# Attention slots of a decoder layer: projections and out-projections issued ahead of the weighted values, and the general arm's transfers on ScalarE's queue

## The chip, the core and the metric

The kernel runs on one core of one Trainium2 chip. A core has TensorE (PE; its weight loads are listed apart as PEld), VectorE (DVE), ScalarE (ACT), GpSimd (POOL) and SyncE (SP), which run side by side and wait for one another through semaphores. Each engine takes its instructions in the order in which the program lists them. The metric is the time of one execution on the device in microseconds (us), lower being better.

## The reference, cut to what matters

One pre-norm decoder layer on `x` of 4 batches, 1024 tokens and 256 features, all fp32: windowed self-attention, cross-attention to 77 context tokens, and a feed-forward block whose activations and weights are rounded to int8 steps. Both attentions have 16 heads of 16 features.

```python
x = x + attn(layernorm(x))                        # self, windows of 128 tokens
x = x + xattn(layernorm(x), ctx_1024, mask)       # cross, 77 keys
x = x + ffn(layernorm(x))

def attn(x):                                      # per batch and head
    q, k, v = split(x @ w_qkv)
    # a chunk of 128 queries sees its own chunk and the one before, causally
    scores = q_chunk @ concat(k_prev_chunk, k_chunk).T / 4
    return merge(softmax(where(causal, scores, -inf)) @ concat(v_prev, v)) @ w_out

def xattn(x, ctx):
    q, k, v = x @ Wq.T + bq, ctx @ Wk.T + bk, ctx @ Wv.T + bv
    return merge(softmax(where(mask == 0, -inf, q @ k.T / 4)) @ v) @ Wo.T + bo

def ffn(x):
    h = fake_quant(silu(fake_quant(x) @ Wg.T) * (fake_quant(x) @ Wu.T))
    return h @ Wd.T          # one quantisation scale over all of x, one over all of h
```

The mask that is drawn here has the same row for every query.

## The kernel before, in words

The attention part treats eight jobs in turn: self-attention ("S") of batches 0, 1 and 2, cross-attention ("X") of batch 0, S of batch 3, X of batches 1, 2 and 3. A job is cut into units `(job, g, o, u)`: `g` and `o` pick four heads, whose score products run in four row groups of TensorE at once, and `u` picks two tiles of 128 tokens (S, four values) or half of the tokens (X, two values). That makes 96 units.

The work is written out as a loop over **slots**, one for each unit. `tc.manual_schedule(engines=None)` keeps every engine's instructions in the order in which this loop emits them. A slot of the steady state emits, in this order:

1. for the units that `values_of` lists, **the weighted values**: `weighted_values` (32 or 40 products into the bank `ps_av`, L854, for S; 4 long ones, L864, for X; then a VectorE transpose from the bank, L878), `normalise` (reciprocal L886 and product L888 on VectorE) and, for `o == 1`, `by_features` (a second VectorE transpose, L900). An S job has these in every second slot, an X job in every slot;
2. **the tasks** that are due: `project` (q and k, `ps_p`, L304, taken out of the bank by two ScalarE instructions, L363, L367 or L369), `values` (`ps_v`, one ScalarE copy, L696), `out_project` (`ps_op`, added to `x` by VectorE, L918), `normed_T` (the transposes `ps_t`), and the weights' preparation. `next_in` picks them by due slot and by a cost limit for each slot;
3. **pieces set beside** (`beside`): VectorE work on statistics (L192, L194), on the quantisation of the feed-forward weights (L598 to L608) and on the third norm's maxima (L949);
4. `put_maxima`, where a group of heads is complete: its negated maxima go through TensorE, a ScalarE copy and four transfers on SyncE's queue into the spare rows of `q`;
5. `maxima` for the unit five slots ahead (`LEAD = 5`): scores into the four banks `sc_n` (L725, L740), reduced by VectorE to maxima (L755: eight pairs of instructions for S; L766: four for X);
6. `weights` of the slot's own unit: scores into the four banks `sc_t` (L810, L839), exponentials by ScalarE (L820, L842), a causal selection by GpSimd (L824).

All PSUM banks come from one pool of eight under one tag, `tag="b"`, and are handed out in turn. So the first bank that a slot asks for is the one that held the first `sc_n` of the slot before, the second one that of the second `sc_n`, and so on; the last ones that it asks for (the last `sc_t`) are those that it took first.

The last `LEAD` slots (`tail`) and the slot after the last unit have code of their own.

`values` writes into five tiles `vtiles`, used in turn; `values` for the second pair of token tiles of a job goes into the tile that the job before last read in its weighted values.

Whether all mask rows are alike is found out at the start; `tc.If(rows_alike != 0)` then runs `attention(True)` and `feed_forward()`, or, in the general arm, `attention(False)` and `feed_forward()`. Both arms are in the program, and the first is the one that runs here. Transfers are issued by SyncE but for the last two output blocks, which ScalarE issues (L1522), and for accumulating ones by GpSimd.

Of the kernel before, what the change touches and what calls it, by code (L numbers as in the profile page):

```python
# [25 lines left out]
def decoder_layer(  # L26
# [175 lines left out]
    with ExitStack() as att:  # L202
# [204 lines left out]

        begun = dict(turn)
        begin.close()

        def attention(alike):
            turn.update(begun)
            arm = ExitStack()
            wp = arm.enter_context(tc.tile_pool(name="wa", bufs=1))
            stage = arm.enter_context(tc.tile_pool(name="stage", bufs=2))
# [21 lines left out]
            def prep_cross():  # L437
# [4 lines left out]
                def load_biases():  # L442
                    with nc.allow_non_contiguous_dma(reason="256-element biases"):
                        for name, src in (("q", bq), ("k", bk)):
                            raws[name] = small.tile([P, NP], F32, name="raw_b")
                            nc.sync.dma_start(out=raws[name], in_=src.rearrange("(g p) -> p g", p=P))
                    nc.sync.dma_start(out=bv_b, in_=bv.partition_broadcast(SK))
                    nc.sync.dma_start(out=bo_b, in_=bo.partition_broadcast(P))

                def biases():  # L450
                    for name, dst, by, plus in (("q", bq_p, qrows, nextrow), ("k", bk_p, rows, onerow)):
# [6 lines left out]
                def transposed(w, name, dst=None):  # L458
                    def load():
                        raws[name] = stage.tile([P, NC, D], F32, name="raw_w", tag="stage")  # L460
                        nc.sync.dma_start(out=raws[name], in_=w.rearrange("(c p) i -> p c i", p=P))

                    def turn():
                        wx[name] = dst
                        if dst is None:
                            wx[name] = work.tile([P, NC, D], F32, name=name, tag="wkv", bufs=1)
                        for ic in range(NC):
                            ps = bank("ps_w")
                            for oc in range(NC):
                                nc.tensor.transpose(  # L470
                                    ps[:, oc * P : (oc + 1) * P],
                                    raws[name][:, oc, ic * P : (ic + 1) * P],
                                    ident,
                                )
                            nc.vector.tensor_copy(wx[name][:, ic, :], ps[:, 0:D])

                    return [load, turn]

                def load_context():
                    raws["c"] = stage.tile([SK, B, D], F32, name="craw", tag="stage")  # L480
                    nc.sync.dma_start(out=raws["c"], in_=ctx_in.rearrange("b k d -> k b d"))

                def context():
                    for c in range(NC):
# [51 lines left out]

                def load_row():
                    raws["m"] = stage.tile([P, SK], I32, name="mrow", tag="stage")
                    nc.sync.dma_start(out=raws["m"], in_=mask[0, :].partition_broadcast(P))

                def add_row():

                    row = raws["r"] = stage.tile([P, SK], F32, name="brow", tag="stage")
                    nc.vector.tensor_scalar(row, raws["m"], 0.0, NEG, ALU.is_equal, ALU.mult)
                    least = small.tile([P, 1], F32, name="least")
                    nc.vector.tensor_reduce(least, row, AX.X, ALU.max)
                    nc.vector.tensor_scalar(least, least, -NEG, None, ALU.mult)
                    nc.vector.tensor_tensor(nokey, least, least, ALU.subtract)
                    for o in range(NS):
                        for g in range(NP):  # L550
                            at = (1 - o) * HD + 1
                            nc.sync.dma_start(
                                out=kx[at : P : SL, g, o, :].rearrange("j (b k) -> j b k", b=B),
                                in_=row[0:NJ].unsqueeze(1).to_broadcast([NJ, B, SK]),
                            )

                def load_mask():
                    raws["m"] = stage.tile([P, NT, SK], I32, name="mraw", tag="stage")
                    nc.sync.dma_start(out=raws["m"], in_=mask.rearrange("(t p) k -> p t k", p=P))

                def mask_bias():
                    nc.vector.tensor_scalar(mb_n, raws["m"], 0.0, NEG, ALU.is_equal, ALU.mult)
# [47 lines left out]
            def prep_ffn():  # L610


                def rows_of(w, dst, sc, f):
                    kept = {}

                    def load():
                        kept["raw"] = stage.tile([P, D], F32, name="raw_f", tag="stage")
                        if f < NF - 1:
                            nc.sync.dma_start(out=kept["raw"], in_=w[f * P : (f + 1) * P, :])
                        else:  # L620
                            for r in (0, HR):
                                nc.sync.dma_start(out=kept["raw"][r : r + HR], in_=w[f * P :, :])

                    def scale():
                        kept["i"] = row_scale(kept["raw"], P, sc[:, f : f + 1])

                    def quant():
                        kept["q"] = stage.tile([P, D], BF16, name="q_f", tag="stage_q")
                        quantise_rows(kept["raw"], P, kept["i"], kept["q"])

                    def turn():
                        ps = ps_b.tile([P, NC, P], BF16, name="ps_f", tag="b")
                        for c in range(NC):
                            nc.tensor.transpose(
                                ps[:, c, :], kept["q"][:, c * P : (c + 1) * P], ident_bf
                            )
                        nc.vector.tensor_copy(dst[:, :, f * P : (f + 1) * P], ps)

                    return [load, scale, quant, turn]

                def down(c):
                    kept = {}

                    def load():
                        kept["raw"] = stage.tile([P, FF], F32, name="raw_d", tag="stage")
                        nc.sync.dma_start(out=kept["raw"], in_=w_down[c * P : (c + 1) * P, :])

                    def scale():
                        kept["i"] = row_scale(kept["raw"], P, dsc[:, c : c + 1])
# [124 lines left out]
            def put_maxima(job, g, o):  # L774

                ps = bank("ps_mx")
                nc.tensor.transpose(
                    ps[: NJ * NT, :P], job.mx[g, o].rearrange("p j t -> p (j t)"), ident
                )
                mxT = work.tile([NJ * NT, P], F32, name="mxT", tag="mxT", bufs=2)  # L780
                nc.scalar.copy(mxT, ps[: NJ * NT, :P])
                for j in range(NJ):
                    row = j * SL + (1 - o) * HD
                    nc.sync.dma_start(
                        out=job.q[g, o][row : row + 1, :],
                        in_=mxT[j * NT : (j + 1) * NT, :],
                    )
# [335 lines left out]
            for j, job in enumerate(jobs):  # L1123
# [58 lines left out]
                            values_of.setdefault(at, []).append((job, g, o, hf))  # L1182
                if S_:
                    for t2 in range(NT // 2):
                        a, by = ((-3, -1) if j else (-1, -1), (-1, 1), (3, 3), (4, 4))[t2]
                        task(t0 + a, t0 + by, 1.0, values, job, t2)
                then = jobs[j + 1].kind if j + 1 < len(jobs) else ""
                for hf in range(NH):
# [25 lines left out]
            for slot in range(first, last):  # L1214
# [6 lines left out]
                if slot == N:  # L1221
# [11 lines left out]
                        while after:  # L1233
                            after.pop(0)()
                    last_project(jobs[-1])
                else:
                    for args in values_of.get(slot, ()):
                        weighted_values(*args)
                        normalise(*args, tail)
                        if not tail:  # L1240
                            by_features(*args)
                spent = 0.0
                cap = 1.35 if now and ahead else 2.3
                while t := next_in(tasks, slot, spent, cap):
                    spent += t[3]
                    fn, args = t[4:]
                    fn(*args)
                    if fn is out_project:
                        job, hf, t2 = args
                        if job.kind == "X" and t2 == HT // 2 - 1:  # L1250
                            third_norm(job.b, hf, slot)
                spent = 0.0
                while t := next_in(beside, slot, spent, 1.2):
                    spent += t[3]
# [25 lines left out]
        def feed_forward():  # L1280
# [149 lines left out]
            def rows_out(t0):  # L1430
                b, t = divmod(t0, NT)
                return out[b, t * P : (t + 2) * P, :].rearrange("(t p) d -> p t d", p=P)
# [1 line left out]

            added_there = {t0 for t0 in range(0, B * NT - 4, 2) if t0 % 4 == 0}
            for t0 in sorted(added_there):
                nc.sync.dma_start(out=rows_out(t0), in_=xb[t0 // NT][:, t0 % NT : t0 % NT + 2, :])

            ins = [Input(0), Input(1)]
            ins[0].quantise(2, HT, nc.vector)  # L1440
# [56 lines left out]
            def down(q, t0, nt):  # L1497
                odd = t0 // HT % 2
                for t2 in range(nt // 2):
# [19 lines left out]
                        nc.gpsimd.dma_start(out=rows_out(t0 + 2 * t2), in_=y, accum_op=ALU.add)  # L1519
                    else:  # L1520
                        nc.vector.tensor_tensor(y, y, xb[b][:, t : t + 2, :], ALU.add)
                        (nc.scalar if t0 + 2 * t2 >= B * NT - 4 else nc.sync).dma_start(  # L1522
                            out=rows_out(t0 + 2 * t2), in_=y
                        )


            parts = [(0, 2), (2, 2)] + [(i * HT, HT) for i in range(1, NB - 1)]
# [67 lines left out]
```

## Time and profile before

| | us |
|---|---|
| median of 3 runs | 665.53 (665.24 to 666.23) |
| the profiled execution's own time | 663.93 |
| its span, first to last instruction | 662.1 |
| TensorE / VectorE / ScalarE / GpSimd busy | 613.3 / 542.7 / 367.6 / 268.8 |
| granted TensorE clock, mean | 0.99 |

The profile is of one execution. "Busy" is the union of an engine's instructions; matmuls are pipelined and their ends are modelled. In the views of waits each line names who waited, for whom, the total in us, how often, and the longest. In the timeline each row has the start in us, the length, the engine, the line of the kernel, the operation, its tiles, how many were merged, and the idle time before it with what ended it. The attention slots fill about 31 to 540 us of the span, the feed-forward block the rest.

### The profile page before, as it was taken

To read this page: it belongs to the slowest core of one execution; us is meant where nothing else is said; L and a number is where in the kernel's file an instruction comes from. 1 tells how busy PE (TensorE), PEld (TensorE's weight loads), DVE (VectorE), ACT (ScalarE), POOL (GpSimd) and SP (SyncE) were. 2 spreads that over 40 slices of the span, in tenths; PEclk is the share of its full clock that TensorE was granted. 3 is DMA by queue.
4 is the path that set the end of the run, shared out by engine and by line. 5 is a ranking of instruction groups with operands and counts; after the bars stand their busy time and mean duration, and the time that the engine had idled before them with its cause. 6 is when DMAs were issued, how large, how long until landed. Compare 5 with 4: busy or idle time off the path is not lost.

```text
span 662.1 us, 20220 instructions
## 1 busy us (share of the span) xinstructions
PE 613.3 (93%) x7857; PEld 350.9 (53%) x7862; DVE 542.7 (82%) x1922; ACT 367.6 (56%) x672; POOL 268.8 (41%) x520
## 2 busy tenths in 40 slices
PE   9899999999999999999999999999999997787775
PEld 6456566566555665654446666544443445333564
DVE  6878778868779799678997996897978787889896
ACT  2365564644555634645565366447556475788392
POOL 3164533647234667650044867526611141111032
PEclk9999999999999999999999999999999999989899
DMA  8100100000000000000000000000000020000057
GB/s 291 48 4 15 38 3 2 18 5 5 18 27 10 12 2 19 9 15 14 8 10 11 12 24 26 5 3 4 3 2 4 4 96 17 1 0 1 0 97 165
DMA packets 18080, 17.43 MB, mean 26 GB/s; under 512 B 2998, under 2 KB 17335, under 8 KB 17975
## 3 DMA queue, kind: packets, MB, share of 16 engines
q1 hardware_dynamic: 15239, 13.69, 6.4%
q0 software_dynamic: 1904, 1.84, 2.1%
q8 instruction: 64, 1.05, 0.7%
q10 hardware_dynamic: 832, 0.53, 0.3%
q14 instruction: 41, 0.34, 0.2%
HBM read 9.47 MB, written 6.03 MB: 23 GB/s over the span
## 4 chain that ended last, share of the span: by engine, by line
PE 61%; DVE 25%; ACT 7%; issue 5%; POOL 1%; DVEq 0%; ACTq 0%
PE ps_p L304 13%; PE ps_av L854 8%; PE sc_t L810 7%; PE sc_n L725 7%; PE ps_op L304 6%; PE ps_av L864 4%; PE sc_t L839 3%; DVE junk L755 3%; PE ps_v L304 3%; PE sc_n L740 3%; DVE bnst L192 2%; DVE o_sb L878 2%; ACT shared L369 2%; PE ps_idle L117 2%; DVE aT L900 2%
## 5 line engine op out<-in xcount | busy, mean ns | idle before, releaser
L755 DVE CUSTOM_DVE_ANT_0 junk<-sc_n,cboth 128x256 bf16<-128x256 f32 (+1 forms) x512 | 172.3, 402 | 35.1 <-PE sc_n L725 35.1
L820 ACT ACTIVATE pt<-sc_t 128x512 f32<-128x512 f32 (+1 forms) x256 | 125.4, 577 | 85.3 <-PE sc_t L810 85.3
L824 POOL TENSOR_SCALAR_AFFINE_SELECT pt<-pt 128x256 f32<-128x256 f32 x256 | 102.2, 407 | 116.1 <-ACT pt L820 105.5
L810 PE MATMUL sc_t<-shared 32*128 32x256 f32 (+1 forms) x1024 | 87.9, 377 | 1.4 <-DVE vx L530 0.3
L842 ACT ACTIVATE ptx<-sc_t 77x512 f32<-77x512 f32 x128 | 65.2, 596 | 37.0 <-PE sc_t L839 37.0
L725 PE MATMUL sc_n<-shared 32*128 32x256 f32 (+1 forms) x1024 | 73.6, 387 | 3.0 <-ACT shared L369 1.6
L810 PEld LDWEIGHTS sc_t<-shared 32*128 32x128 f32 x1024 | 65.5, 185 | 13.6 <-ACT shared L367 3.2
L320 POOL TENSOR_SCALAR xn<-x,mv,rs 128x256 f32<-128x256 f32 x56 | 69.6, 1249 | 0.0
L160 POOL TENSOR_SCALAR ve<-mv 128x4 f32<-128x4 f32 x20 | 4.6, 232 | 153.8 <-DVE mv L194 153.7
L878 DVE STREAM_TRANSPOSE o_sb<-ps_av 128x512 f32<-128x512 f32 x63 | 45.0, 714 | 24.4 <-PE ps_av L854 14.3
L304 PE MATMUL ps_p<-shared,w_s 128*32 128x512 f32 x512 | 60.9, 595 | 3.4 <-DVE mx L766 1.6
L725 PEld LDWEIGHTS sc_n<-shared 32*128 32x128 f32 x1024 | 45.7, 184 | 32.3 <-DVE mx L755 10.8
L854 PE MATMUL ps_av<-pt,vt 128*32 128x256 f32 (+1 forms) x1152 | 59.3, 349 | 3.0 <-DVE mx L755 2.6
L766 DVE TENSOR_REDUCE mx<-sc_n 128x4 f32<-128x308 f32 x128 | 51.8, 466 | 8.5 <-PE sc_n L740 8.3
L854 PEld LDWEIGHTS ps_av<-pt,vt 128*32 128x32 f32 x1152 | 34.9, 110 | 31.5 <-DVE mx L755 6.4
L839 PE MATMUL sc_t<-shared,kx 32*77 32x512 f32 x256 | 45.9, 599 | 0.0
L755 DVE DVE_READ_ACCUMULATOR2_ANT mx<- 128x1 f32 x512 | 42.4, 83 | 0.1
L864 PE MATMUL ps_av<-ptx,vx 77*32 77x512 f32 x256 | 35.9, 605 | 3.4 <-DVE mx L766 2.5
L363 ACT ACTIVATE shared<-ps_p,bq_p,qrows 128x512 f32<-128x512 f32 x32 | 23.1, 773 | 26.0 <-PE ps_p L304 26.0
L740 PEld LDWEIGHTS sc_n<-kx,shared 32*128 32x128 f32 x1024 | 31.7, 186 | 10.2 <-DVE rec L886 1.7
L740 PE MATMUL sc_n<-kx,shared 32*128 32x77 f32 x1024 | 36.5, 277 | 0.0
L1406 ACT ACTIVATE act<-pg,gsc 128x512 f32<-128x512 f32 x44 | 29.2, 687 | 11.4 <-PE pg L1391 6.3
(201 smaller groups left out, 984.8 us busy)
## 6 DMA issues: line engine op xcount, KB each, us to landing
x<-in_x_dram SPq DMA_DIRECT2D x8, 512.0 KB
shared<-mxT SPq DMA_DIRECT2D x128, 4.0 KB
out_dram<-x SPq DMA_DIRECT2D x7, 256.0 KB
out_dram<-shared POOLq DMA_DIRECT2D x7, 256.0 KB, 4.6
out_dram<-shared SPq DMA_DIRECT2D x7, 256.0 KB
w_s<-in_L_attn_w_qkv_dram SPq DMA_DIRECT2D x2, 384.0 KB
raw_d<-in_L_ffn_w_down_dram SPq DMA_DIRECT2D x2, 352.0 KB
raw_f<-in_L_ffn_w_gate_dram SPq DMA_DIRECT2D x5, 128.0 KB
```

The costliest lines, as they stand in the source:

```text
L304: nc.tensor.matmul(out[r], lhsT[:, r], rhs, skip_group_check=True, **on)
L320: eng.tensor_scalar(xn, xb[job.b][:, t, :], job.st[hf].mv[:, i, 0:1], job.st[hf].rs[:, i : i + 1], ALU.subtract, ALU.mult,)
L725: nc.tensor.matmul(banks[j][:, (i + 1) * 2 * P - n : (i + 1) * 2 * P], q[r, t * P : (t + 1) * P], k[r, k0 * P : k0 * P + n], start=True, s ...
L740: nc.tensor.matmul(banks[j][:, i * SK : (i + 1) * SK], q[r, t * P : (t + 1) * P], k[r, :], start=alike, stop=alike or i == HT - 1,)
L755: nc.vector.tensor_tensor_reduce(out=junk[:, 2 * P - n :], in0=banks[j][:, (i + 1) * 2 * P - n : (i + 1) * 2 * P], in1=cboth[:, 2 * P - n ...
L810: nc.tensor.matmul(banks[j][:, w : w + n], k[r, t * P : (t + 1) * P], q[r, t * P : t * P + n], start=True, stop=True,)
L820: nc.scalar.activation(pt.rearrange("p i a q -> p (i a q)")[:, :w], banks[j][:, :w], AF.Exp)
L824: nc.gpsimd.affine_select(out=pt[:, :, 0, :], in_=pt[:, :, 0, :], compare_op=ALU.is_ge, fill=0.0, base=0, pattern=[[0, 2], [1, P]], channe ...
L839: nc.tensor.matmul(banks[j][:SK], k[r, :], q[r, s], start=alike, stop=True)
L842: nc.scalar.activation(pt, banks[j][:SK], AF.Exp)
L854: nc.tensor.matmul(ps[j * SL : (j + 1) * SL, (a0 - t0) * P : (a1 - t0) * P], slot_of(job.vs[kb // 2][:, kb % 2], heads[j]), job.pts[g, o, ...
L864: nc.tensor.matmul(ps[j * SL : (j + 1) * SL, :], slot_of(vx[:, job.b], heads[j]), job.pts[g, o, j, hf], start=True, stop=True,)
```

## The change

- In the steady state the weighted values of a slot (`weighted_values`, `normalise`, `by_features`) are emitted after the slot's tasks. They still stand ahead of the pieces set beside, of `put_maxima`, `maxima` and `weights`. The tail is as it was.
- The task `values` for the second pair of token tiles may be done in slot 0 or 1 of its job and no earlier (before: from one slot ahead of it).
- A variable `queue_of` holds the queue for transfers: SyncE's in the arm that runs here, ScalarE's in the general arm. Every `nc.sync.dma_start` of `attention` and `feed_forward` goes through it. With that the last two output blocks of the arm that runs go by SyncE.

```diff
+        queue_of = [nc.sync]
 
         def attention(alike):
             turn.update(begun)
+            queue_of[0] = nc.sync if alike else nc.scalar
...
-                    nc.sync.dma_start(
+                    queue_of[0].dma_start(
                         out=job.q[g, o][row : row + 1, :],
                         in_=mxT[j * NT : (j + 1) * NT, :],
                     )
...
                     for t2 in range(NT // 2):
-                        a, by = ((-3, -1) if j else (-1, -1), (-1, 1), (3, 3), (4, 4))[t2]
+                        a, by = ((-3, -1) if j else (-1, -1), (0, 1), (3, 3), (4, 4))[t2]
                         task(t0 + a, t0 + by, 1.0, values, job, t2)
...
                     last_project(jobs[-1])
-                else:
+                elif tail:
                     for args in values_of.get(slot, ()):
                         weighted_values(*args)
                         normalise(*args, tail)
-                        if not tail:
-                            by_features(*args)
                 spent = 0.0
                 cap = 1.35 if now and ahead else 2.3
                 while t := next_in(tasks, slot, spent, cap):
...
                             third_norm(job.b, hf, slot)
+                if not tail:
+                    for args in values_of.get(slot, ()):
+                        weighted_values(*args)
+                        normalise(*args, tail)
+                        by_features(*args)
                 spent = 0.0
                 while t := next_in(beside, slot, spent, 1.2):
                     spent += t[3]
...
                         nc.vector.tensor_tensor(y, y, xb[b][:, t : t + 2, :], ALU.add)
-                        (nc.scalar if t0 + 2 * t2 >= B * NT - 4 else nc.sync).dma_start(
-                            out=rows_out(t0 + 2 * t2), in_=y
-                        )
+                        queue_of[0].dma_start(out=rows_out(t0 + 2 * t2), in_=y)
```

More of the change, by code (lines that the diff above doesn't have):

```diff
@@ L445, in load_biases @@
                             raws[name] = small.tile([P, NP], F32, name="raw_b")
-                            nc.sync.dma_start(out=raws[name], in_=src.rearrange("(g p) -> p g", p=P))
-                    nc.sync.dma_start(out=bv_b, in_=bv.partition_broadcast(SK))
-                    nc.sync.dma_start(out=bo_b, in_=bo.partition_broadcast(P))
+                            queue_of[0].dma_start(out=raws[name], in_=src.rearrange("(g p) -> p g", p=P))
+                    queue_of[0].dma_start(out=bv_b, in_=bv.partition_broadcast(SK))
+                    queue_of[0].dma_start(out=bo_b, in_=bo.partition_broadcast(P))
                 def biases():
@@ L460, in load @@
                         raws[name] = stage.tile([P, NC, D], F32, name="raw_w", tag="stage")
-                        nc.sync.dma_start(out=raws[name], in_=w.rearrange("(c p) i -> p c i", p=P))
+                        queue_of[0].dma_start(out=raws[name], in_=w.rearrange("(c p) i -> p c i", p=P))
                     def turn():
@@ L480, in load_context @@
                     raws["c"] = stage.tile([SK, B, D], F32, name="craw", tag="stage")
-                    nc.sync.dma_start(out=raws["c"], in_=ctx_in.rearrange("b k d -> k b d"))
+                    queue_of[0].dma_start(out=raws["c"], in_=ctx_in.rearrange("b k d -> k b d"))
                 def context():
@@ L538, in load_row @@
                     raws["m"] = stage.tile([P, SK], I32, name="mrow", tag="stage")
-                    nc.sync.dma_start(out=raws["m"], in_=mask[0, :].partition_broadcast(P))
+                    queue_of[0].dma_start(out=raws["m"], in_=mask[0, :].partition_broadcast(P))
                 def add_row():
@@ L558, in load_mask @@
                     raws["m"] = stage.tile([P, NT, SK], I32, name="mraw", tag="stage")
-                    nc.sync.dma_start(out=raws["m"], in_=mask.rearrange("(t p) k -> p t k", p=P))
+                    queue_of[0].dma_start(out=raws["m"], in_=mask.rearrange("(t p) k -> p t k", p=P))
                 def mask_bias():
@@ L618, in load @@
                         if f < NF - 1:
-                            nc.sync.dma_start(out=kept["raw"], in_=w[f * P : (f + 1) * P, :])
+                            queue_of[0].dma_start(out=kept["raw"], in_=w[f * P : (f + 1) * P, :])
                         else:
                             for r in (0, HR):
-                                nc.sync.dma_start(out=kept["raw"][r : r + HR], in_=w[f * P :, :])
+                                queue_of[0].dma_start(out=kept["raw"][r : r + HR], in_=w[f * P :, :])
                     def scale():
@@ L645, in load @@
                         kept["raw"] = stage.tile([P, FF], F32, name="raw_d", tag="stage")
-                        nc.sync.dma_start(out=kept["raw"], in_=w_down[c * P : (c + 1) * P, :])
+                        queue_of[0].dma_start(out=kept["raw"], in_=w_down[c * P : (c + 1) * P, :])
                     def scale():
@@ L783, in put_maxima @@
                     row = j * SL + (1 - o) * HD
-                    nc.sync.dma_start(
+                    queue_of[0].dma_start(
                         out=job.q[g, o][row : row + 1, :],
@@ L1436, in feed_forward @@
             for t0 in sorted(added_there):
-                nc.sync.dma_start(out=rows_out(t0), in_=xb[t0 // NT][:, t0 % NT : t0 % NT + 2, :])
+                queue_of[0].dma_start(out=rows_out(t0), in_=xb[t0 // NT][:, t0 % NT : t0 % NT + 2, :])
             ins = [Input(0), Input(1)]
```

## The prediction

> **What bounds the kernel now.** I read the page's busy shares first, then the attention stretch of the table by windows, then the timeline slot by slot.
>
> ```profile
> PE 613.3 (93%) x7857; PEld 350.9 (53%) x7862; DVE 542.7 (82%) x1922; ACT 367.6 (56%) x672; POOL 268.8 (41%) x520
> ```
> ```profile
> 32.00:540.00 508.00, 492.50 (x6936) 274.63 (x6933) 416.14 (x1645) 280.61 (x553) 237.08 (x463) 1.00 0.05 14
> ```
>
> In the attention slots TensorE shows 492.5 us busy of 508 and VectorE 416.1. Only 15.5 us look idle, but "busy" also covers matmuls that wait inside a group: the groups of `sc_t` take between 1.0 and 2.0 us for the same work. So I measure a slot from the start of its first product to the start of the next slot's. This is a common slot with weighted values and a projection:
>
> ```profile
> 119.16 1.94 PE L854 MATMUL ps_av<-pt,vt 128*32 128x128 f32 x40
> ...
> 120.92 1.90 PE L304 MATMUL ps_p<-shared,w_s 128*32 128x512 f32 x16
> 121.22 0.72 DVE L878 STREAM_TRANSPOSE o_sb<-ps_av 128x512 f32<-128x512 f32 x1 [0.59 <-PE ps_av L854]
> ...
> 122.72 0.71 DVE L900 STREAM_TRANSPOSE aT<-aN 128x512 f32<-128x512 f32 x1
> ...
> 122.75 1.15 PE L725 MATMUL sc_n<-shared 32*128 32x256 f32 x16
> 122.94 1.45 ACT L369 ACTIVATE shared<-ps_p,onerow,rows 128x512 f32<-128x512 f32 x2 [1.96 <-PE ps_p L304]
> ...
> 123.71 1.85 PE L810 MATMUL sc_t<-shared 32*128 32x256 f32 x16
> 123.91 0.42 DVE L755 CUSTOM_DVE_ANT_0 junk<-sc_n,cboth 128x256 bf16<-128x256 f32 x1 [0.48 <-PE sc_n L725]
> ...
> 125.49 1.92 PE L304 MATMUL ps_p<-shared,w_s 128*32 128x512 f32 x16
> ```
>
> Two things are to be seen. First, VectorE's chain for the weighted values (121.22 to 123.33: transpose, reciprocal, product, second transpose) lies wholly beside the projection and the scores; VectorE even waits 0.48 us for `sc_n`. Secondly, `sc_t` runs late: its last bank is the one that the projection used, and ScalarE empties that only at 124.39. Scores and `sc_t` take 122.75 to 125.49, 2.74 us; in slots where nothing waits they take 0.97 + 1.03 = 2.00 (those that end in `ps_v`, as from 98.52 to 104.11). So 0.74 us are lost here.
>
> The second reading is a slot in which, today, no task stands behind the weighted values:
>
> ```profile
> 282.79 1.72 PE L854 MATMUL ps_av<-pt,vt 128*32 128x256 f32 x32
> ...
> 284.61 0.72 DVE L878 STREAM_TRANSPOSE o_sb<-ps_av 128x512 f32<-128x512 f32 x1 [1.51 <-PE ps_av L854]
> ...
> 284.66 1.13 PE L740 MATMUL sc_n<-kx,shared 32*128 32x77 f32 x32
> ...
> 286.11 0.71 DVE L900 STREAM_TRANSPOSE aT<-aN 128x512 f32<-128x512 f32 x1
> ...
> 287.09 0.57 DVE L608 CAST q_f<-w 128x256 bf16<-128x256 int8 x1
> ...
> 287.58 1.61 DVE L766 TENSOR_REDUCE mx<-sc_n 128x4 f32<-128x308 f32 x4
> ...
> 288.10 1.50 PE L304 MATMUL ps_p<-shared,w_s 128*32 128x512 f32 x12 [1.61 <-DVE mx L766]
> ```
>
> The scores are ready by 285.8, but VectorE must first finish the chain (284.61 to 286.74) and the piece set beside (to 287.58). The next slot's first product needs the first `sc_n` bank, so TensorE stands still for 1.61 us until the first reduction is done. That is the order that the change gives to every such slot.
>
> **The change part by part.**
>
> *The weighted values behind the tasks.* The products are the same, so TensorE's own work costs nothing more. The moved steps issue no transfer, nothing on ScalarE and, outside the tail, nothing on GpSimd, so those queues and SyncE's keep their order. On VectorE the transpose L878 now waits for a product that ends later by the tasks' length; behind it queue the rest of the chain, the pieces beside and the reductions, and for the first reduction waits TensorE's next slot (and later `put_maxima`).
>
> I count the wait of each slot after the change from rows. From the end of the weighted values to the start of VectorE's chain: 0.26 us (S; 121.22 less 119.16 + 1.75, L878 only; 0.13 in X with its short products). The chain: 0.72 + 0.25 + 0.42 and gaps = 1.45 us for `o == 0`, 2.15 with L900. The pieces beside: 0.85 (statistics), 0.7 to 0.8 (row scale), 0.65 (L607 and L608), 1.4 (maxima L949), as the slot has them. From the first reduction's start to the next slot's first product: 0.82 us in S (two pairs of L755, then the hand-over), 0.51 in X (287.58 to 288.10). Against this, TensorE itself needs 2.0 us from the end of the weighted values to the end of the slot, 2.2 in X with `put_maxima`, 1.9 in S with it.
>
> There are 53 slots in the steady state with weighted values and tasks. In four classes, the mean wait after, with the pieces beside summed from VectorE's rows between chain and first reduction:
>
> - S, short chain, 15 slots: 0.26 + 1.45 + 0.44 + 0.82 - 1.94 = 1.03; before 0.23
> - S, long chain, 15: 0.26 + 2.15 + 0.55 + 0.82 - 1.94 = 1.84; before 0.54
> - X, short chain, 13: 0.14 + 1.47 + 0.95 + 0.51 - 2.07 = 1.00; before 0.46
> - X, long chain, 10: 0.14 + 2.16 + 1.11 + 0.51 - 2.07 = 1.85; before 0.67
>
> The sum is 15.5 + 27.6 + 13.0 + 18.5 = 74.6 us of waits after. Those of before in the same slots, slot length less unhindered length, are 3.5 + 8.1 + 6.0 + 6.7 = 24.3. The difference is **+50.3 us**. What the change takes away is in it: 12.4 us of the 24.3 are the 19 slots that end in a projection, whose bank ScalarE will now empty under the weighted values. The 0.74 at 119.16 goes, and 0.26 + 2.15 + 0.82 - 2.00 = 1.23 comes: what is late next is VectorE.
>
> The sum's bounds: if half of the 38 us of pieces beside found cover, 19 less, +31; a slot in which a projection already waits 1.7 us inside (476.61 to 485.58) may give that back. Upwards stands the clock:
>
> ```profile
> 64.90:71.00 6.10, 6.02 (x83) 3.90 (x79) 5.28 (x29) 2.32 (x5) 4.09 (x9) 0.72 0.02 4
> ```
>
> Here the granted clock was 0.72 over 6.1 us, which is half speed for 3.4 us, right after the slot from 62.38 to 67.36 that lost 2.98 us; slots that lost 1.3 to 1.5 show no such drop. Thirteen of the slots above come to 2.0 to 2.55 us, in between. If each brought such a stretch, 13 x 1.7 = 22 us more at most. I take zero, since most are nearer to 1.45 and 2.0 than to 2.98, and keep half of it for the range. [...]
>
> *`values` no earlier than slot 0.* Four products of 1.85 us with a ScalarE copy of 0.59 move by a slot or two, for instance from 109.26 to 119.16. The work is the same, and TensorE and ScalarE do it under the same scores: nothing, within 0.5 us each way. Both slots keep their chain, so a wait in the one is as long as I counted.
>
> *The queue variable.* In the arm that runs it changes the last two output blocks alone. ScalarE issues these now in 0.40 us each, SyncE takes 0.37. SyncE leaves the arm at 655.3 and its next instruction stands at 659.7, 4.3 us for a taken jump, hidden while the last blocks land. After the change it leaves about 658.0. With the same 4.3 us it would come to its final waits at 662.3, some 2.0 us later at the end; with no such cost, nothing. I take the middle, +1.0. [...]
>
> *Sum:* 663.93 + 50.3 + 1.0 = 715.2 against the profiled execution. The median of the runs lies 1.6 above that execution, so the forecast is **716.8 us**.
>
> **The rivals.**
>
> *Faster.* Where the next slot's first product does not have to wait for VectorE, only ScalarE's late emptying counts, and with it the 12.4 us of the 19 slots go: 653. The point that decides is the time from the end of the weighted values to the first reduction: chain and pieces must fit into 2.00 - 0.26 - 0.82 = 0.92 us (S) or 2.07 - 0.14 - 0.51 = 1.4 (X). For it speaks VectorE's 18% of idle time; against it the shortest chain, 1.45.
>
> *Only the chain is exposed,* because the pieces beside run while VectorE waits for the products: the four classes without their pieces give 36 us of waits, +12, so 678. Against it: the pieces are emitted behind the chain, and VectorE keeps that order.
>
> *The clock drops as well:* with all 22 us, 739.
>
> *No effect:* the reordering would have to leave VectorE's order alone; it does not, since the op additions now stand ahead of the transposes.
>
> **How the numbers follow.** The forecast as it stands has 0.80, the clock rival 0.07, the chain alone 0.07, faster 0.04, no effect 0.02. The range reaches from +31 (698) to +50 with half the clock's term and the jump in full (730). A change of 0.2%, 1.3 us, is about what a measurement of this kernel can tell from none. Faster 0.04, same 0.02, slower 0.94.
>
> **What would show it.** TensorE's waits for `mx` ahead of the first product of a slot should grow from single microseconds to some 60 or 70 in all; the chain L878 of a slot should follow its weighted values at once and the first L755 come 1.5 to 3 us after; `sc_t` with a projection in the slot should fall to about 1.05 us; VectorE's wait for `ps_av` should grow from 22 us to over 60, its busy time staying at 543. I am wrong if the slots with weighted values are no longer than before, or if the span grows by less than 30 us.

## The result and the profile after

The changed kernel takes 713.97 us (median of 4 runs, 710.35 to 719.67) against 665.75 us (4 runs, 665.24 to 666.23): ratio 1.0724, 95% interval 1.0671 to 1.0778. The forecast of 716.8 us lies 2.8 us above the median and inside the spread of the runs. The profiled execution took 716.08 us, with a span of 714.3. That is 52.2 us more than before: the attention slots, which ended at 537.50 us, end at 589.25, and what follows takes 125.0 us against 124.6.

The line of the page with the busy times, then the attention stretch from the table by windows:

```profile
PE 611.5 (86%) x7862; PEld 346.1 (48%) x7862; DVE 543.0 (76%) x1922; ACT 369.6 (52%) x672; POOL 266.9 (37%) x520
```
```profile
31.00:592.00 561.00, 493.04 (x6981) 270.53 (x6982) 417.58 (x1651) 283.74 (x555) 235.28 (x464) 0.98 0.04 13
```

TensorE's and VectorE's busy times are those of before (493.0 after 492.5, 417.6 after 416.1), in a stretch that is 53 us longer. So no engine has more to do; both wait for each other. The waits, each with its total, number and longest, say on what:

```profile
DVE o_sb L880 <- PE ps_av L856: 59.1, 30, 4.0
DVE o_sb L880 <- PE ps_av L866: 22.5, 19, 2.6
PE ps_p L304 <- DVE mx L757: 16.7, 14, 1.9
```

VectorE waits 81.6 us for the weighted values, where it waited 22.3. The third line is one of several in which TensorE's next first product waits for a reduction; all lines of the view on such a wait come to 63.1 us, before the change to 12.0 (without the one for `ps_mx`, which is no slot's first product). The slot that answers to the one shown from 119.16 is this one, in the timeline of the changed kernel (it has a `values` product more, by the second part of the change):

```profile
123.55 1.92 PE L304 MATMUL ps_p<-shared,w_s 128*32 128x512 f32 x16
...
125.29 1.91 PE L304 MATMUL ps_v<-w_s,shared 128*32 128x256 f32 x32
...
127.02 1.92 PE L856 MATMUL ps_av<-pt,vt 128*32 128x128 f32 x40
...
128.87 1.15 PE L727 MATMUL sc_n<-shared 32*128 32x256 f32 x16
129.06 0.72 DVE L880 STREAM_TRANSPOSE o_sb<-ps_av 128x512 f32<-128x512 f32 x1 [4.01 <-PE ps_av L856]
...
129.83 1.12 PE L812 MATMUL sc_t<-shared 32*128 32x256 f32 x16
...
130.55 0.71 DVE L902 STREAM_TRANSPOSE aT<-aN 128x512 f32<-128x512 f32 x1
...
131.19 0.39 DVE L757 CUSTOM_DVE_ANT_0 junk<-sc_n,cboth 128x256 bf16<-128x256 f32 x1
...
131.99 0.64 PE L304 MATMUL ps_p<-shared,w_s 128*32 128x512 f32 x4 [1.04 <-DVE mx L757]
```

VectorE stands still for 4.01 us beside the projection, the values and the weighted values, and then has its chain (129.06 to 131.19) all in a row, with TensorE already through the scores. `sc_t` takes 1.12 us instead of 1.85: ScalarE's late emptying is gone. The next slot's first product comes at 131.99, 1.04 us late, after the first two pairs of L757.

The clock did what the forecast had set at zero. The same out-projection in TensorE's timeline before, then its surroundings in the timeline of the changed kernel, and that stretch in the table by windows:

```profile
417.37 1.93 PE L304 MATMUL ps_op<-wo_s,aT 128*32 128x256 f32 x32 [0.21 <-DVE mx L766]
```

```profile
453.63 1.13 PE L742 MATMUL sc_n<-kx,shared 32*128 32x77 f32 x32
454.58 0.88 PE L812 MATMUL sc_t<-shared 32*128 32x256 f32 x16
457.84 3.64 PE L304 MATMUL ps_op<-wo_s,aT 128*32 128x256 f32 x32 [2.38 <-DVE mx L768]
461.41 2.01 PE L742 MATMUL sc_n<-kx,shared 32*128 32x77 f32 x32
```
```profile
456.00:468.00 12.00, 10.16 (x105) 4.74 (x106) 6.07 (x17) 3.22 (x8) 6.40 (x9) 0.57 0.01 1
```

After a wait of 2.38 us the same products take 3.64 instead of 1.93 us, and the granted clock is 0.57 over 12 us, which is half clock for 10.2 of them. By the record of the granted clock, 27.3 us pass at half clock in the attention slots, 3.4 before.

### The profile page after: what moved, and what is told of

Same layout as the page of the kernel before. It is cut to its first block, busy times and chain, and to the rows that moved or that the text cites. A ratio compares the mean times of both kernels' runs of the same rounds, so it can differ in the third digit from the quotient of the medians.

```text
span 714.3 us, 20230 instructions
## 1 busy us (share of the span) xinstructions
PE 611.5 (86%) x7862; PEld 346.1 (48%) x7862; DVE 543.0 (76%) x1922; ACT 369.6 (52%) x672; POOL 266.9 (37%) x520
## 3 DMA queue, kind: packets, MB, share of 16 engines
q0 software_dynamic: 1904, 1.84, 2.0%
## 5 line engine op out<-in xcount | busy, mean ns | idle before, releaser
L757 DVE CUSTOM_DVE_ANT_0 junk<-sc_n,cboth 128x256 bf16<-128x256 f32 (+1 forms) x512 | 172.1, 402 | 17.4 <-PE sc_n L727 17.4
L880 DVE STREAM_TRANSPOSE o_sb<-ps_av 128x512 f32<-128x512 f32 x63 | 45.1, 715 | 83.5 <-PE ps_av L856 59.1
L727 PE MATMUL sc_n<-shared 32*128 32x256 f32 (+1 forms) x1024 | 76.5, 393 | 3.1 <-DVE mx L757 1.4
L812 PE MATMUL sc_t<-shared 32*128 32x256 f32 (+1 forms) x1024 | 78.4, 377 | 0.6 <-DVE kx L510 0.3
L812 PEld LDWEIGHTS sc_t<-shared 32*128 32x128 f32 x1024 | 61.6, 188 | 7.0 <-ACT shared L367 1.4
L757 DVE DVE_READ_ACCUMULATOR2_ANT mx<- 128x1 f32 x512 | 42.6, 83 | 0.1
L304 PE MATMUL ps_op<-wo_s,aT 128*32 128x256 f32 x512 | 33.7, 407 | 9.9 <-DVE mx L757 5.2
L304 PE MATMUL ps_p<-shared,wq_x 128*32 128x512 f32 x256 | 31.8, 616 | 8.7 <-DVE mx L768 7.0
L841 PE MATMUL sc_t<-shared,kx 32*77 32x512 f32 x256 | 38.4, 610 | 0.0
L304 PEld LDWEIGHTS ps_p<-shared,w_s 128*32 128x32 f32 x512 | 13.8, 109 | 49.2 <-DVE mx L757 24.5
```

Of the source, the lines that this page charges most:

```text
L304: nc.tensor.matmul(out[r], lhsT[:, r], rhs, skip_group_check=True, **on)
L727: nc.tensor.matmul(banks[j][:, (i + 1) * 2 * P - n : (i + 1) * 2 * P], q[r, t * P : (t + 1) * P], k[r, k0 * P : k0 * P + n], start=True, s ...
L757: nc.vector.tensor_tensor_reduce(out=junk[:, 2 * P - n :], in0=banks[j][:, (i + 1) * 2 * P - n : (i + 1) * 2 * P], in1=cboth[:, 2 * P - n ...
L812: nc.tensor.matmul(banks[j][:, w : w + n], k[r, t * P : (t + 1) * P], q[r, t * P : t * P + n], start=True, stop=True,)
L841: nc.tensor.matmul(banks[j][:SK], k[r, :], q[r, s], start=alike, stop=True)
L880: nc.vector.transpose(job.av[g, o, hf], ps)
```

## The experiments

In all of them "the 53 slots" are those of the prediction, and a slot is measured in the timeline from its first product to that of the next. Its wait is the time from the start of `sc_t` to the next slot, less the 1.03 us that `sc_t` takes when nothing waits (0.90 in S slots with `put_maxima`, which keep it shorter). By this measure the 53 slots wait 24.2 us before and 60.7 us in the changed kernel. Where it says what the others take, the start up to the second slot is counted with them.

**The reordering without the queues.**

```
+            queue_of[0] = nc.sync      (in both arms)
+            (nc.scalar if t0 + 2 * t2 >= B * NT - 4 else nc.sync).dma_start(...)   (as before)
```

> The changed kernel with its queue edits undone: the weighted values stand behind the tasks, and values is due from slot 0, but SyncE and ScalarE issue the output blocks as before. Theory (the reordering alone puts VectorE's chain and the pieces beside it between the weighted values and the next slot): the time of the changed kernel, 714 us within 710 to 720, with the attention slots again some 51 us longer than before and VectorE waiting some 82 us for ps_av. Prediction's own term for the queues: 1.0 us less than that, 713. Rival (the queues carry a real share): below 705.

Measured: 714.64 us (711.77 to 720.12), ratio 1.0746 (1.0711 to 1.0781). The waits of the 53 slots are 60.5 us, class by class within 0.1 us of the changed kernel. The reordering with its `values` edit is the whole loss. The reordering with `values` left as it was has not been run.

**The queues without the reordering.**

> The kernel of before with the queue variable alone: SyncE issues all output blocks of the arm that runs. Prediction's term: +1.0 us (between 0 and +2.0), 666.8, with SyncE's end instruction 4.3 us behind its last jump. What the changed kernel's trace suggests (SyncE's last branch at 710.2, its next instruction at 710.4): no such cost, 665.7 within 0.7 us. Rival (ScalarE or SyncE delayed by the transfers): over 668.

Measured: 664.92 us, ratio 0.9985 (0.9973 to 0.9997). The term of +1.0 us is wrong in sign. The source view of the program's last line, before and here, gives the first and last start of SyncE's instructions there:

```profile
L1591 SPq EVENT_SEMAPHORE  x14: 17/28/28, 659.7 to 662.1; - x14
```
```profile
L1591 SPq EVENT_SEMAPHORE  x14: 17/28/28, 657.7 to 661.9; - x14
```

SyncE's last branch stands at 655.3 before and at 657.5 here. It took 4.3 us to its next instruction there, and 0.2 us here.

**The pieces beside ahead of the weighted values.**

```
-  if not tail: weighted_values, normalise, by_features
-  pieces beside
+  pieces beside
+  if not tail: weighted_values, normalise, by_features
```

> The changed kernel with the pieces beside emitted ahead of the weighted values, so that VectorE does them while it waits for ps_av. Theory (chain and pieces together stand between the weighted values and the first reduction): of the 38 us of pieces in the 53 slots most find cover, the waits at the ends of these slots fall from 61 to 25 to 35 us, the half-clock stretches in the attention part from 27 us to under 10; the time is 675 to 688. Rival 'only the chain is exposed': the pieces are already covered, so nothing changes, 710 to 716. Rival 'VectorE has no room': the pieces now delay the op additions or the chain, 714 or more.

Measured: 684.24 us (683.67 to 685.36), ratio 1.0283 (1.0263 to 1.0304). The waits of the 53 slots fall from 60.7 to 34.9 us, and VectorE's own wait shrinks:

```profile
DVE o_sb L880 <- PE ps_av L856: 41.3, 24, 4.0
DVE o_sb L880 <- PE ps_av L866: 11.1, 10, 2.0
```

So the pieces were exposed, as the theory says and the rival "only the chain" denies. TensorE's order is unchanged here, and 30 us are gone. The half-clock time in the attention slots falls from 27.3 to 6.8 us along with the waits.

**Zeros in the place of waits, everywhere.**

```
+  if not tail and slot in values_of:
+      idle(ahead[0].nb[0], 6)
```

> The changed kernel with six products of zeros (about 0.11 us each at full clock, 0.65 us) written into the first score bank ahead of the real scores in the slots with weighted values: TensorE is busy for a part of the time that it would otherwise wait. The result is the same. Theory with the clock as a real share (27 us at half clock in the attention part, worth 8 to 12 us): a slot that waits 0.65 us or more is no longer for it, the half-clock stretches go to under 10 us, the time is 703 to 710. Rival (the clock has no share, the waits alone carry all): slots with waits of less than 0.65 us become longer, 714 to 725.

Measured: 719.41 us (717.87 to 722.20). The expected gain was missed. The six products take 0.82 us in the trace, not 0.65, and a slot that waits less than that gets longer. Between 386 and 470 us, however, the fourteen slots take 8.5 us more than before instead of 18.3, so the experiment was repeated there alone.

**Zeros in seven slots.** The same, `and slot in range(61, 74)`.

> The changed kernel with the six products of zeros (0.82 us of TensorE) in only seven slots with weighted values, the ones from 386 to 470 us that wait over 1 us each. Theory with the clock: no half-clock stretch is left between 390 and 470 us (23.9 us in the changed kernel's profile), these fourteen slots take 9 to 10 us more than before instead of 18.3, and the time is 705 to 710 with a narrower spread than 710 to 720. Rival (the filled slots get longer by the filling, the clock has no share): 714 to 720.

Measured: 710.45 us (707.19 to 712.07), ratio 1.0669 (1.0645 to 1.0693): just above the theory's range and below the rival's; the spread is 5 us. The same place in its timeline:

```profile
449.43 0.82 PE L117 MATMUL sc_n<-zeros 128*128 128x256 bf16 x6
450.18 1.13 PE L742 MATMUL sc_n<-kx,shared 32*128 32x77 f32 x32
451.13 0.88 PE L812 MATMUL sc_t<-shared 32*128 32x256 f32 x16
453.66 1.93 PE L304 MATMUL ps_op<-wo_s,aT 128*32 128x256 f32 x32 [1.66 <-DVE mx L768]
455.52 1.13 PE L742 MATMUL sc_n<-kx,shared 32*128 32x77 f32 x32
```

From the weighted values' end (449.38) to 453.66 it takes 4.28 us, against 4.35 without the filling; only the wait inside is 0.72 us shorter, and the products after it run at full clock. No half-clock stretch is left between 386 and 471 us, and the fourteen slots take +8.5 us against +18.3 in the changed kernel's profile and +10.7 in that of the reordering without the queues. The clock is a term of its own, worth about 10 us in the profiled execution and 3.5 to 4.2 in the medians (713.97 and 714.64 against 710.45). The ratio's interval lies clear of that of the reordering without the queues (from 1.0711) and just overlaps that of the changed kernel (from 1.0671).

**The chain behind the reductions.** Only L880 stays ahead of them; `normalise`, `by_features` and the pieces are emitted behind `maxima`.

> The changed kernel, but of the weighted values' chain only the first transposition stays ahead of VectorE's reductions; reciprocal, product, second transposition and the pieces beside are emitted behind them. Theory (TensorE's next slot waits for whatever VectorE does between the weighted values and the first reduction): what is left there is 0.1 + 0.72, and with 0.68 to the hand-over that is 1.5 us against 2.0 of TensorE's own work, so the waits of the 53 slots nearly vanish, 61 to under 15 us, and ScalarE's late emptying stays away too: 640 to 665. Rival (VectorE's work is only pushed into the next slot and is late there): 670 to 700. Rival (TensorE's order itself costs the time, whatever VectorE does): 710 or more.

Measured: 681.84 us (679.14 to 689.05), ratio 1.0220 (1.0199 to 1.0241). The 53 slots now wait 7.5 us, less than before the change, so the place of VectorE's work was what they paid for. But the other slots take 20.0 us more than before, above all those just behind: +2.5 at the `t` slot from 258.9 and +3.5 at the `op` slot from 417.4 (times of before), which have no weighted values of their own. (`t` stands for a slot whose task is `normed_T`, `op` for one with `out_project`.) The rival held: the work is late in the next slot. Part of the 20 is the clock, at half for 23.9 us between 355 and 490 us of this profile, whose execution was the slowest of the runs (689.05); the second of these two slots has 3.4 us of it, the first none.

**The pieces behind the reductions in the old order.**

> The kernel of before with the pieces beside emitted behind the reductions. Theory: of the 24 us that the 53 slots wait before, some 12 are ScalarE's late emptying and stay, the other 12 are VectorE's and go in part: 655 to 663. Rival (pieces late in the next slot): 665 to 672.

Measured: 664.88 us, ratio 0.9994 (0.9981 to 1.0008): no difference, and the theory's 655 to 663 is missed. Slots gain up to 1.18 us, and the next ones give it back. In the old order the place of the pieces is worth nothing.

**The self-attention jobs alone.**

> The changed kernel with the weighted values behind the tasks only for the self-attention jobs; those of the cross-attention jobs stand ahead of the tasks as before. By the prediction's classes S brings 3.5 + 8.1 before against 43.1 after, +31.5, X the rest, +18.8; by the changed kernel's trace S brings +28 without the clock and X +14.5. So 693 to 699 with little at half clock in the cross-attention stretch. Rival (one kind carries it all): 666 or 714.

Measured: 697.44 us (696.15 to 706.33), ratio 1.0518 (1.0468 to 1.0569). In its profile the attention slots take 31.4 us more than before. The waits of the self-attention classes rise by 22.4 us of that; half clock lasts 13.7 us against 3.4.

**`values` due from slot 0, nothing else.**

```
-  a, by = (..., (-1, 1), (3, 3), (4, 4))[t2]
+  a, by = (..., (0, 1), (3, 3), (4, 4))[t2]
```

> The kernel of before with values due from slot 0 alone; weighted values and queues as before. Prediction's term: 665.5 us, within 0.5. Rival (a value product that stands behind the weighted values is what hides VectorE's chain there, as at 109.26 and 197.9 us before: without it such a slot waits, while the product costs its 1.85 us in a later slot): +1 to +2 us for each of two jobs, 667 to 670.

Measured: 671.62 us (668.50 to 675.39), ratio 1.0075 (1.0049 to 1.0102). Neither the prediction's 0.5 nor the rival's upper edge covers it. Rows of TensorE and VectorE in the slot that began at 109.26 before with weighted values, `values` and `put_maxima`, and is now without `values`:

```profile
115.26 0.72 DVE L878 STREAM_TRANSPOSE o_sb<-ps_av 128x512 f32<-128x512 f32 x1 [0.23 <-PE ps_av L854]
...
116.76 0.71 DVE L900 STREAM_TRANSPOSE aT<-aN 128x512 f32<-128x512 f32 x1
...
118.24 0.26 DVE L755 CUSTOM_DVE_ANT_0 junk<-sc_n,cboth 128x128 bf16<-128x128 f32 x1
...
118.91 2.84 PE L304 MATMUL ps_p<-shared,w_s 128*32 128x512 f32 x16 [1.96 <-DVE mx L755]
```

The slot is as long as it was with the product (5.5 us), since the chain and the pieces set its end; TensorE now waits 1.96 us instead. The product costs 1.0 us in the slot where it went, and here the wait is followed by a stretch at half clock (2.84 instead of 1.92 us for the projection). The slots that changed place add up to some 3 us, half-clock stretches to some more; how much of the 5.2 us is which is not settled by one profile. The runs help: the two at the highest clock (0.994 and 0.992) took 668.83 and 668.50 us, where the kernel of before at 0.993 took 665.51 and 666.57. So some 2 to 3 us are there with little of the clock's part.

**Pieces first and the chain behind.**

> The changed kernel with the pieces beside ahead of the weighted values, the first transposition right behind these, and reciprocal, product and second transposition behind the reductions. Theory (what VectorE does between the weighted values and the first reduction is paid, and what it does behind the reductions is paid in the next slot only where that one has no slack): the waits of the 53 slots go to under 10 us as with the chain behind, and of the 20 us that other slots then lost the pieces' share goes: 660 to 674. Rival (it is the chain behind the reductions that is late, not the pieces): 678 to 685.

Measured: 673.03 us (671.79 to 675.46), ratio 1.0108 (1.0084 to 1.0132). The 53 slots wait 8.8 us, the others take 14.2 us more than before. By the ratios it beats the version with both behind by 7.5 us, so something of the pieces' share came back. Part of the difference is the clock, at half for 6.8 us of these slots against 30.7 there. The rest of the chain is still late in the next slot.

**Pieces first and the second transposition behind.**

> As the run with the pieces ahead of the weighted values (684.2 us), but with the second transposition alone (0.71 us, in every second pair) behind the reductions. Theory: the slots with the long chain lose what it took, 17.9 + 9.1 us of waits go to about 10, and little is pushed into the next slot: 668 to 676. Rival (it comes back in full in the next slot): 682 to 686.

Measured: 674.84 us (672.89 to 675.77), ratio 1.0128 (1.0105 to 1.0152). The slots with the long chain fall from 27.0 to 9.6 us of waits, and the other slots take 4.2 us more than before, with the pieces first alone 3.3.

**The new order where it pays.**

```
+  PICK = {7, 43, 45, 47, 61, 69, 71, 74, 75, 79, 82, 83, 86}
-  else: weighted_values, normalise, by_features; tasks; pieces
+  slot in PICK:  tasks; pieces; weighted_values, normalise, by_features
+  other slots:   as before
```

> The kernel of before, with the moved order (pieces beside, then weighted values, both behind the tasks) only in the thirteen slots where the run with the pieces first had a shorter slot than before and the next slot did not give it back. By those slots' lengths in the two traces (-0.67, -0.20, -0.30, -0.89, -0.31, -0.64, -0.11, -0.13, -0.36, -0.33, -0.22, -0.67, -0.60, and +0.40 behind one): 5.0 us less than before, 660 to 662. Rival (a slot's time depends on where VectorE stands from the slots before, so the lengths do not carry over): 664 to 667.

Measured: 662.96 us (661.23 to 663.95) against 666.38, ratio 0.9947 (0.9928 to 0.9966). It is faster than the kernel of before by 3.4 us (2.3 to 4.8 by the interval) where 5.0 were expected, and lies between the theory's range and the rival's. Of the thirteen slots twelve gain, each to within 0.03 us of what it had gained in the run with the pieces first (-0.86 at 281.9, -0.67 at 473.3, -0.60 at 493.2, for instance); one that had gained 0.20 gains nothing. The attention slots end 4.4 us earlier, but in this profile what follows takes 126.4 us against 124.6.

## Why the prediction was right, and where it was not

The sign and the mechanism were right. The time was right partly by luck, because errors cancel: one term was too large, and what had been set at zero or left out makes up for it. Against the profiled execution's +52.2 us:

- *The waits of the 53 slots:* forecast 74.6 after less 24.3 before, +50.3; measured 60.7 less 24.2, **+36.5**. The term was 14 us too large. By the kernel's rule (`o == 1` has the long chain) the classes hold 16, 14, 12 and 11 slots, not 15, 15, 13 and 10, which leaves the sum at 74.6. Their means were 0.83, 1.63, 0.73 and 1.43 us against 1.03, 1.84, 1.00 and 1.85. The start of the chain was mis-sized most in S: 0.26 us was read from one slot (the difference written there gives 0.31; from the end of its row of weighted values, 121.10, it is 0.12), and the changed kernel shows 0.07 to 0.15, mean 0.10. The bare chain takes 1.38 and 2.13 us, not 1.45 and 2.15, and the hand-over in S slots with `put_maxima` is 0.66 to 0.69, not 0.82. In the class of X slots with the long chain such terms explain little of the 0.42 us, and TensorE's own work measures 2.02 there, not more than the 2.07 of the forecast. The rest is taken up below.
- *The clock:* forecast 0, with a bound of 22. Measured **about +10** in the profiled execution (18.3 less 8.5 us in the fourteen slots), 3.5 to 4.2 in the medians. This step failed. It reasoned from one stretch behind a loss of 2.98 us, took most of its 2.0 to 2.55 as safe, and put half of the bound into the range. But the record of the granted clock has that stretch from 65.46 to 68.87 us, so it began inside the slot (62.38 to 67.36), and part of the 2.98 us was its effect: up to `sc_t` at 64.99 TensorE had lost only 1.6 us (64.99 less 62.38 + 0.97). In the changed kernel four drops came with waits of 1.87 to 2.38 us.
- *`values`:* forecast 0, within 0.5. By itself it costs 5.2 us, some of it by the clock, so the reason given for it was wrong: where the product went into a slot it was not "under the same scores" at no cost, and where it left, it had been hiding VectorE's chain. With the weighted values behind the tasks it could not hide the chain any more in either place, so in the sum it should already be in the two slots' waits; this is argued, since the reordering was not run without it.
- *SyncE's end:* forecast +1.0; alone the queues give -0.6 us (0.9985), and in the changed kernel SyncE's last branch at 710.2 is followed by its next instruction at 710.4. The step took half of what the 4.3 us would cost. In the two kernels whose SyncE has the transfers of the general arm the jump takes some 4.3 us (655.3 to 659.7 before, 702.2 to 706.5 in the reordering without the queues), in the two where it has none 0.2 (657.5 to 657.7 with the queues alone, 710.2 to 710.4 in the changed kernel). What makes the difference, no run shows.
- *What the forecast left out:* +0.35 us at the start, +0.45 behind the attention slots, and by difference some 5 us elsewhere in the attention part, among them +0.6 at `t` slots right behind a long one and +1.5 net in the first three slots whose products changed place.

36.5 + 9.8 + 5.1 + 0.8 = 52.2, where 5.1 is what the other terms leave.

Most of what is missing in that last class lies in two slots, from 510.25 and 535.68 us, whose pieces take 1.4 us. The count gives them some 2.1 us each, and they wait 0.67. In the timeline of the changed kernel, at the end of the first:

```profile
515.62 1.93 PE L304 MATMUL ps_op<-wo_x,aT 128*32 128x256 f32 x32 [0.66 <-ACT ptx L844]
516.78 1.63 DVE L768 TENSOR_REDUCE mx<-sc_n 128x4 f32<-128x308 f32 x4
```

The next slot's first product waits for an exponential and starts ahead of the reduction. So a slot's first bank is not always that of the first `sc_n` of the slot before; why not here, no run shows.

The split by kind looks close, S by the classes +31.5 and 31.4 measured over the attention slots with S alone. That too is luck, since only 22.4 us of it are the waits that the classes count. Of the signs, TensorE's waits for `mx` (63.1 us, though from 12.0 and not from single microseconds), `sc_t` (1.12 us), the chain right behind the weighted values, VectorE's wait (81.6 us) and its unchanged busy time came as named. Of the rivals, "only the chain exposed" is refuted by the pieces-first run: the pieces are worth 30 us, 25.8 of them in the 53 slots' waits, and the half-clock time falls along with these. "The clock drops as well" is true in part. "Faster" fails at its own point: chain and pieces do not fit under 0.92 and 1.4 us. But its other half is real, since ScalarE's late emptying went away, and in chosen slots the moved order gains. Not all of that gain is ScalarE's: two of the twelve slots (from 67.36 and 282.79 us before) have no task on TensorE, and their 0.64 and 0.86 us come from the place of the pieces alone.

## What to carry to other kernels

Ask of two engines that feed each other not what is busy but what lies, on the second engine, between the last product it needs and the first result that the first engine waits for: that stretch has to fit under the first engine's remaining work, slot by slot. A task that stands behind a hand-over is a cover for it; moving it ahead can cost as much as it had hidden, and moving work out of the stretch only pays if the next slot has room for it. A reordering that loses as a rule can gain in single slots, and slot lengths read from two traces carried over to a mixed version within 0.03 us in twelve slots of thirteen, though the whole gained 3.4 us and not 5.0.

## What the hardware showed that was not expected

Waits of TensorE of 1.8 to 2.4 us were followed by half clock in some cases and not in others. In the changed kernel's attention slots eight waits are longer than 1.8 us, and four of them brought a drop. In the run of the reordering alone a wait of 1.87 us at 393.29 brought none, where the changed kernel's 1.87 at 393.39 did; 1.88 us at the same place (416.81 and 419.66) brought one in both. The stretches last 3.41 us or a multiple (6.83, 10.24). The spread of the changed kernel's runs is this: at clocks of 0.981, 0.980, 0.975 and 0.968 they took 710.35, 711.86, 716.08 and 719.67 us.

The place of the stretches is regular, too. In the profile before, the first three starts (65.46, 584.28 and 625.24 us) lie 152 and 12 times 3.413 us apart; in the changed kernel's attention slots (67.82, 395.50, 409.15, 422.81 and 456.94 us) it is 96, 4, 4 and 10 times that. This alone does not tell which wait brings a drop: the two of 1.87 us each lie wholly between two points of such a grid (392.09 and 395.50 in the changed kernel, 391.80 and 395.22 in the reordering alone), and one brought a drop.
